# One receptance product in float32r parts, the norms' scaling on VectorE, and a planner that charges first weight loads by place

## The chip, the cores and the metric

The kernel runs on one core of a Trainium2 chip. A core has five engines that work side by side, each through its own queue in order: TensorE (PE in the profile; its weight loads are listed as PEld), VectorE (DVE), ScalarE (ACT), GpSimd (POOL) and SyncE (SP), which here issues all transfers. Products of TensorE land in PSUM, in banks of 128x512 float32. Everything else lives in SBUF, or in device memory. The metric is the time of one execution in device microseconds (us).

## What is computed

The input is x of 8 sequences by 1024 tokens by 256 channels, float32. Four blocks follow one another, each with a layer norm in front and a residual sum behind:

```python
x = x + retention(layernorm(x))      # its own norm inside, 4 heads, chunked state, gated, + its input
x = x + ffn(layernorm(x))
x = x + attention(layernorm(x))      # 16 heads, T5-style relative bias, softmax
x = x + ffn(layernorm(x))            # the same weights as the first ffn
```

The feed-forward block (ffn) mixes each token with the one before it and gates its output by a "receptance" r:

```python
xr = mu_r * x + (1 - mu_r) * x_prev
xk = mu_k * x + (1 - mu_k) * x_prev
r  = sigmoid(xr @ W_r.T)
out = r * (square(relu(xk @ W_k.T)) @ W_v.T)
```

The attention block projects q, k and v with biases, adds a bias by distance to the scores, takes a softmax over 1024 keys and projects back.

## The kernel before, in words

**Tiles and stages.** Tokens go in chunks of 256 (`CT`; four chunks, `NC`, per sequence), as tiles of 128 partitions by 2 by 256 channels. For each of 8 sequences `b` the program records: `retention(b)`, the first feed-forward block (`ffn_front`, which calls `ffn_chunk` once per chunk), `project_b` (norm and q, k, v projections of the attention), eight passes of `maxima` (scores once, for the row maximum, tiles `p`), four of `weigh` (scores again, exponentials, weighted values, tiles `s`, `e` and `acc`), and `back(b)` (output projection and the second feed-forward block, `ffn_chunk` again). So `ffn_chunk` runs 64 times: 8 sequences, 4 chunks, two blocks.

**Norms.** `moments` takes mean and variance on DVE, `rstd` and `power` the inverse root on POOL, `product` the shift. `normed` then writes the scaled tile `z` with two ACT operations of 128x256 (scale and bias per token); `turn_chunk` scales the residual `xc` the same way. `turned` transposes `z` on PE into PSUM (`ntp`, `ftp`, `btp`). In `turn_chunk` four ACT operations then read `ntp` and apply the inner norm's weights, two for the rounded part `nT[0]`, two for the full value in `z`; `nT[1]` is their difference.

**Products in two formats.** Some weights and inputs are kept as two float32r parts, a rounded one and what is left. `mm3` then makes one product from three: low by high, high by low, high by high. The projections of retention and attention (`qps`, `vps`, `gps`, `qkp`, `bvp`) are such products. Those of the feed-forward block (`kps`, `rps`, `yps`) and the output projections (`wps`, `bop`) are plain float32. `rps`, the receptance, is four float32 products of 128x256 per chunk, with tokens as the stationary operand; ACT takes its tanh.

**q and k of the attention.** In `project_b`, per chunk and per q or k, two ACT operations add the bias from PSUM into `res`, one ACT operation rounds it to the part `qk0`, and POOL (DVE for the first sequence, by `swift`) subtracts to the part `qk1`. SP then stores the parts to `stk`, from where `load_pair` brings them back per pair of heads as `q` and `k`.

**PSUM.** Seven banks under the tag `one` are shared by all products but `acc`, which has its own. A bank comes free when the last engine has read it: DVE (`pm`, `jmax`) for `p`, ACT (`e`) for `s`.

**What sets the order.** Nothing is issued as it is recorded. A planner (`Plan`) records every operation with an engine, a cost in microseconds (`estimate`; for products the argument `cost` of `mm` and `turn`), what it must wait for, and a target time. `issue` then walks a clock: whenever an engine is free in its model, it takes the ready operation with the least key (the target, plus terms for PE from `RULES`, chosen every 20 us by a hex digit of `TURNS`), places its tiles into free slots, and emits it. PE operations have a `mode`: "rows" for products over 64 partitions (`p`, `s`, `aps`), "cols" for `sps`, "acc", and "all" for the rest; a change of mode costs `SWITCH` in the model. The costs never reach the chip; they settle only the order in each engine's queue and which slot a tile gets. Tags in `SHARED` take the first free slot, other tags go round in turn.

**First loads.** `later` issues the loads of weights that come after the first of retention. Those kept in parts go through the staging tile `xo0`: ACT rounds, DVE subtracts.

Every instruction goes through one line of `emit`, line 609 in the profile of before, so groups are told apart by tile names there.

Of the kernel before, what the change touches and what calls it, by code (L numbers as in the profile page):

```python
# [10 lines left out]
F32 = mybir.dt.float32  # L11
F32R = mybir.dt.float32r
# [64 lines left out]

STRETCH = 20
TURNS = (
    "00001700f08ff825e9a10f4bfe3f7f5b737f8bc37b237273e3f16482a6fe755707160591be52e6e5"  # L80
    "788ff00f76ff5fc03fdf6bfdd4ccf65b3b9c0cf84111"
)
SWITCH = 0.1

# [94 lines left out]

SHARED = ("z", "one")
_TOUCHED = {}
LOG = None

# [126 lines left out]
class Plan:  # L312
# [14 lines left out]

    class Op:
        __slots__ = ("eng", "calls", "cost", "tail", "before", "after", "target", "mode", "news",
                     "wait", "ready", "done", "n", "tiles", "out", "group")  # L330

    def __init__(self, ctx, tc):
        self.tiles = []
# [25 lines left out]
    @staticmethod  # L359
    def estimate(eng, method, n, views, kw):  # L360
        if eng == "ACT":
            each = 600.0 if isinstance(kw.get("scale"), View) else 1200.0
            fixed = (0.055 if views[0].t.tag == "e2" else 0.045) if views[1].t.space == "psum" else 0.085
            return fixed + n / each + (0.25 if "accum_out" in kw else 0.1 if "bias" in kw and each > 600 else 0.0)
        if eng == "DVE":
            if method == "reciprocal":
                return 0.1 + n / 160.0
            if method == "tensor_scalar":
                return 0.13 + n / 1920.0

            return 0.07 + n / 960.0 + 0.055 * (method == "scalar_tensor_tensor" and kw["scalar"])
        if n <= 16:
            return 0.28 + (0.22 * n if kw.get("op") == ALU.pow else 0.0)
        if method == "affine_select":
            return 0.1 + n / 1000.0

        return 0.2 + n / (490.0 if len({id(v.t) for v in views[1:]}) > 1 else 650.0)

    def record(self, eng, real, method, args, kw):
# [5 lines left out]
        if method in ("matmul", "transpose"):  # L385
            out, group = outs[0].t, kw.pop("group", None)
            op = self.last
            if op is None or op.group is not group or group is None and op.out[0] is not out:
                op = self.new(eng)
                op.out, op.cost, op.group = [], 0.0, group  # L390
                if args[1].dtype == F32R and args[1].shape[0] == P:
                    op.cost = 0.12
                self.last = op
                k, m = args[1].shape[0], 1
                for n in args[1].shape[1:]:
                    m *= n
                op.mode = ("rows" if k == 64 and m == P else "cols") if k == 64 or m == 64 else "all"
                if out.tag == "acc":
                    op.mode = "acc"
            if out not in op.out:  # L400
                op.out.append(out)
            op.cost += cost
# [55 lines left out]
    def issue(self):  # L458
# [59 lines left out]
        while made < len(ops):  # L518
            progress = False
            for e in names:  # L520
                while free[e] <= now:
# [44 lines left out]
                    queue[e].remove(op)  # L566
                    took = op.cost
                    if e == "PE" and op.mode != mode:
                        took += SWITCH
                        mode, first = op.mode, True  # L570
                    elif e == "PE":

                        took += SWITCH * (first and mode == "rows")
                        first = False
# [38 lines left out]
def layer_kernel(ctx: ExitStack, tc: tile.TileContext, ap: dict, out: bass.AP):  # L613
# [26 lines left out]
    def mm(o, lhsT, rhs, start=True, stop=True, share=1.0, group=None):  # L640
        n = 1
        for d in rhs.shape[1:]:
            n *= d
        pe.matmul(o, lhsT, rhs, start=start, stop=stop, group=group,
                  cost=share * (0.005 + (4 if rhs.dtype == F32 else 1) * max(n, 64) / 2280.0))

    def mm3(o, lhsT, rhs, first, last):

# [65 lines left out]


    mu = const([P, 2, ND], "mu")
    wf = {k: const([P, ND, D], k) for k in ("W_r", "W_k", "W_v")}
    wb = {k: halves([P, ND, D], "b" + k) for k in ("wq", "wk", "wv")}
    wo_b = const([P, ND, D], "wo_b")
    bqk = const([P, 2, ND], "bqk")  # L720
# [12 lines left out]

    def later():
        sp.dma_start(mu, ap["f_mu"])
        for k, t in wf.items():
            sp.dma_start(t, ap["f_" + k].rearrange("(c p) n -> p c n", p=P))

        dve.tensor_scalar(wf["W_v"], wf["W_v"], 0.5, None, ALU.mult)
        for k, w in wb.items():  # L740
            t = tile2k("xo0", 2).rearrange("p (c n) -> p c n", c=ND)
            sp.dma_start(t, ap["b_" + k].rearrange("(c p) n -> p c n", p=P))
# [111 lines left out]
    def normed(xc, mv, rs, name):  # L854

        z = small([P, 2, D], "z", 2)
        nb = product(mv[:, :, 0], rs, name + "_nb")
        for n in range(2):
            act.activation(
                z[:, n], xc[:, n], AF.Identity, scale=rs[:, n : n + 1], bias=nb[:, n : n + 1]  # L860
            )
        return z

    def rows_in(ap2, c):
# [10 lines left out]
    def retention(b):  # L875
# [20 lines left out]
        def turn_chunk(c):  # L896
# [1 line left out]
            t = xc[b, c]  # L898
            z = normed(t, mv, rz, "a")
            for n in range(2):  # L900
                act.activation(
                    t[:, n], t[:, n], AF.Identity, scale=s1[:, n : n + 1], bias=m1[:, n : n + 1]
                )
            ps = turned(z, misc("ntp"))
            nT = [tile2k("nT", 2, F32R).rearrange("p (c t) -> p c t", c=ND) for _ in range(2)]
            zT = z.rearrange("p n d -> p (n d)").rearrange("p (c t) -> p c t", c=ND)
            for t in (nT[0], zT):
                for c in range(ND):
                    act.activation(
                        t[:, c], ps[:, c], AF.Identity,  # L910
                        scale=ln[:, 0, c : c + 1], bias=ln[:, 1, c : c + 1],
                    )
            swift(b == 0).tensor_tensor(nT[1], zT, nT[0], ALU.subtract)
            return nT

# [199 lines left out]
    def ffn_chunk(xt, b, ch, name, own):  # L1115
# [28 lines left out]
        def to_tokens(src, w, name):  # L1144
            ps = misc(name)
            for i in range(2):
                for c in range(ND):
# [23 lines left out]
    def project_b(b):  # L1171

        for ch in range(NC):
# [10 lines left out]
            for s, w in ((0, "wq"), (1, "wk")):  # L1184
# [6 lines left out]
                    plan.tile([P, 2, CT], F32R, f"qk{i}", f"qk{i}", 2)  # L1191
                    for i in range(NPART)
                ]
                res = plan.tile([P, 2, CT], F32, "res", "res", 1)
                step = slice(None, None, -1) if s == 0 else slice(None)
                for blk in range(2):
                    bias = bqk[:, s, blk : blk + 1]
                    act.activation(res[:, blk, step], ps[:, blk], AF.Identity, bias=bias)
                act.copy(pt[0], res)
                swift(b == 0).tensor_tensor(pt[1], res, pt[0], ALU.subtract)  # L1200
                t0 = (NC - 1 - ch if s == 0 else ch) * CT
                for p, i in enumerate((Q_PARTS, K_PARTS)[s]):
                    sp.dma_start(rows_of(s, b, t0, p), pt[i].bitcast(F32))
# [106 lines left out]
    def weigh(b, g):  # L1310
# [6 lines left out]
        for hf in (1, 0):  # L1317
# [133 lines left out]
```

## Time and profile before

| | |
|---|---|
| median of 3 runs | 2563.42 us (2562.29 to 2563.48) |
| the profiled execution | 2565.35 us, span 2563.6 us |
| granted TensorE clock, mean | 0.992 |
| busy: PE, PEld | 2477.1 us (97%), 1462.6 us (57%) |
| busy: DVE, ACT, POOL | 2100.9 us (82%), 2071.3 us (81%), 1591.6 us (62%) |
| `rps`, recorded twice for each product | 512 matmuls, 128.6 us |
| `z` on ACT, four groups | 256 operations, 150.5 us |
| bytes moved | 251.18 MB, mean 98 GB/s |

A group's line reads: source line, engine, operation, output and inputs by the program's names with shape and type, count; after the first bar the busy time in us and the mean ns of one; after the second the idle time of the engine just before them, and which work ended most of it. Busy time is the union of the recorded intervals, and the recorded intervals of neighbours can overlap a little, so the spacing of back-to-back instructions is shorter than their mean. The chain is followed backwards from the last instruction, at each step to what released it or to the instruction before it on its engine.

### The profile page before, as it was taken

To read this page: it belongs to the slowest core of one execution; us is meant where nothing else is said; L and a number is where in the kernel's file an instruction comes from. 1 tells how busy PE (TensorE), PEld (TensorE's weight loads), DVE (VectorE), ACT (ScalarE), POOL (GpSimd) and SP (SyncE) were. 2 spreads that over 40 slices of the span, in tenths; PEclk is the share of its full clock that TensorE was granted. 3 is DMA by queue.
4 is the path that set the end of the run, shared out by engine and by line. 5 is a ranking of instruction groups with operands and counts; after the bars stand their busy time and mean duration, and the time that the engine had idled before them with its cause. 6 is when DMAs were issued, how large, how long until landed. Compare 5 with 4: busy or idle time off the path is not lost.

```text
span 2563.6 us, 51515 instructions
## 1 busy us (share of the span) xinstructions
PE 2477.1 (97%) x15814; PEld 1462.6 (57%) x15814; DVE 2100.9 (82%) x6230; ACT 2071.3 (81%) x5334; POOL 1591.6 (62%) x2675
## 2 busy tenths in 40 slices
PE   5998999999999999999999999999999999999997
PEld 3886755555555556555655555555555555554555
DVE  6766988888898888888888888888888888887855
ACT  3564588898989988988889889888998888787783
POOL 3465675666666667766666676666666666665642
PEclk9999999999999999999999999999999999999999
DMA  7136132343424244433234343333243324444322
GB/s 174 42 104 150 55 92 64 92 120 99 111 74 114 78 97 119 123 82 95 71 101 110 98 109 97 89 103 89 81 115 97 101 76 132 120 114 109 92 65 67
DMA packets 252225, 251.18 MB, mean 98 GB/s; under 512 B 89042, under 2 KB 226180, under 8 KB 251924
## 3 DMA queue, kind: packets, MB, share of 16 engines
q1 hardware_dynamic: 251956, 247.89, 35.9%
q8 instruction: 132, 2.16, 0.4%
q14 instruction: 137, 1.12, 0.2%
HBM read 151.32 MB, written 98.59 MB: 97 GB/s over the span
## 4 chain that ended last, share of the span: by engine, by line
PE 78%; DVE 9%; ACT 4%; DMA 3%; POOL 3%; issue 2%; SPq 1%; POOLq 0%; DVEq 0%; ACTq 0%
PE acc L609 16%; PE p L609 10%; PE s L609 10%; PE wps L609 4%; PE yps L609 4%; PE kps L609 4%; PE rps L609 4%; PE gps L609 3%; PE qps L609 3%; DVE pm L609 3%; PE qkp L609 3%; PE vps L609 3%; PE ops L609 3%; ACT e L609 2%; PE bop L609 2%
## 5 line engine op out<-in xcount | busy, mean ns | idle before, releaser
L609 DVE TENSOR_REDUCE pm<-p 128x1 f32<-128x512 f32 (+2 forms) x2048 | 1057.7, 557 | 80.8 <-PE p L609 78.0
L609 ACT ACTIVATE e<-s 128x512 f32<-128x512 f32 (+2 forms) x2048 | 1010.6, 530 | 37.9 <-PE s L609 35.5
L609 POOL TENSOR_TENSOR e<-e,hk 128x512 f32<-128x512 f32 (+1 forms) x558 | 613.1, 1106 | 303.2 <-ACT e L609 296.5
L609 DVE CUSTOM_DVE_ANT_0 jmax<-p,hk 128x256 bf16<-128x256 f32 (+1 forms) x1152 | 427.1, 371 | 122.1 <-PE p L609 117.6
L609 PE MATMUL acc<-e,va 128*17 128x512 f32 x4096 | 524.5, 597 | 0.1
L609 PE MATMUL p<-k,q 64*128 64x512 f32 x2048 | 459.7, 438 | 10.7 <-DMA k<-stk 9.2
L609 ACT COPY e<-s 128x256 f32<-128x256 f32 (+1 forms) x1116 | 402.8, 361 | 83.3 <-PE s L609 80.3
L609 PE MATMUL s<-q,k 64*128 64x512 f32 x2048 | 453.2, 438 | 2.4 <-DVE pm L609 1.0
L609 ACT ACTIVATE e<-e 128x512 f32<-128x512 f32 (+1 forms) x576 | 336.8, 587 | 55.7 <-POOL e L609 52.9
L609 PEld LDWEIGHTS p<-k,q 64*128 64x128 f32 x2048 | 211.0, 185 | 248.2 <-ACT e L609 79.4
L609 PEld LDWEIGHTS s<-q,k 64*128 64x128 f32 x2048 | 205.2, 185 | 203.3 <-issue 63.0
L609 PEld LDWEIGHTS acc<-e,va 128*17 128x17 f32 x4096 | 79.7, 95 | 187.7 <-issue 162.1
L609 PE MATMUL rps<-W_r,xr 128*128 128x256 f32 x512 | 128.6, 393 | 12.8 <-DVE xr L609 10.6
L609 PE MATMUL yps<-W_v,xk 128*128 128x256 f32 x512 | 126.2, 389 | 4.7 <-DVE xk L609 3.4
L609 PE MATMUL wps<-wo_a,gs 128*128 128x256 f32 x512 | 127.4, 392 | 0.9 <-ACT gs L609 0.7
L609 PE MATMUL kps<-xk,W_k 128*128 128x256 f32 x512 | 125.7, 388 | 2.5 <-DVE xk L609 0.9
L609 PEld LDWEIGHTS rps<-W_r,xr 128*128 128x128 f32 x512 | 93.1, 192 | 44.3 <-issue 16.6
L609 PE MATMUL qps<-wqk,nT 128*128 128x512 f32 x384 | 109.4, 421 | 7.1 <-DVE nT L609 5.9
L609 PEld LDWEIGHTS yps<-W_v,xk 128*128 128x128 f32 x512 | 92.2, 190 | 32.1 <-issue 7.7
L609 PEld LDWEIGHTS kps<-xk,W_k 128*128 128x128 f32 x512 | 92.7, 190 | 30.5 <-issue 9.3
L609 PE MATMUL vps<-wv_a,nT 128*128 128x512 f32 x384 | 107.2, 415 | 2.4 <-DVE xc L609 1.8
L609 PEld LDWEIGHTS wps<-wo_a,gs 128*128 128x128 f32 x512 | 93.5, 192 | 25.6 <-ACT e L609 3.4
(182 smaller groups left out, 4135.5 us busy)
## 6 DMA issues: line engine op xcount, KB each, us to landing
stk<-qk SPq DMA_DIRECT2D x192, 256.0 KB
hk<-ud SPq DMA_DIRECT2D x128, 256.0 KB
q<-stk SPq DMA_DIRECT2D x128, 256.0 KB
k<-stk SPq DMA_DIRECT2D x128, 256.0 KB
od<-o SPq DMA_DIRECT2D x64, 256.0 KB
vd<-vst SPq DMA_DIRECT2D x64, 136.0 KB
va<-vd SPq DMA_DIRECT2D x32, 272.0 KB
xc<-in_x SPq DMA_DIRECT2D x32, 256.0 KB
```

The costliest lines, as they stand in the source:

```text
L609: getattr(real, method)(*[be(a) for a in args], **{k: be(a) for k, a in kw.items()})
```

## The change

Six things change.

1. `rps` becomes a product of parts. `W_r` is loaded through `xo0` and kept as two float32r tiles. A new function `parted` makes two tiles from `xr`: `xrh`, rounded, by a DVE copy, and `xrl`, what is left, by a POOL subtraction. `to_tokens` then uses `mm3`, twelve float32r products per chunk in place of four float32 ones. The four tags of the parts go into `SHARED`.
2. `normed` and the residual scaling in `turn_chunk` move from ACT to DVE, as `tensor_scalar` with two scalars per partition.
3. In `turn_chunk` ACT reads `ntp` twice, not four times; DVE copies the full value to the rounded part `nT[0]`.
4. In `project_b`, ACT writes the biased value rounded into `qk0` at once, and DVE subtracts it from PSUM plus bias into `qk1`. The tile `res`, its cast and POOL's subtraction are gone.
5. The planner's costs: DVE operations on SBUF alone, products and their shares, and a term `late` for the first load of weights that is charged when PE changes into mode "all", in place of 0.12 for every group of float32r products over 128 partitions.
6. `TURNS` has other digits.

```diff
-SHARED = ("z", "one")
+SHARED = ("z", "one", "xkh", "xkl", "xrh", "xrl")
...
-            if method == "tensor_scalar":
-                return 0.13 + n / 1920.0
+            if method in ("tensor_scalar", "tensor_copy") and all(v.t.space == "sbuf" for v in views):
+                return 0.07 + n / 1920.0 + 0.055 * kw["scalar"]
...
-                if args[1].dtype == F32R and args[1].shape[0] == P:
-                    op.cost = 0.12
...
+                op.late = (0.055 if method == "transpose" else 0.1) if op.mode == "all" else 0.0
...
-                        took += SWITCH
+                        took += SWITCH + op.late
...
-                  cost=share * (0.005 + (4 if rhs.dtype == F32 else 1) * max(n, 64) / 2280.0))
+                  cost=share * (0.004 + (4 if rhs.dtype == F32 else 1) * max(n, 64) / 2400.0))
...
-    wf = {k: const([P, ND, D], k) for k in ("W_r", "W_k", "W_v")}
+    wf = {k: halves([P, ND, D], k) if k[2] in "r" else const([P, ND, D], k) for k in ("W_r", "W_k", "W_v")}
...
-        for k, t in wf.items():
+        for k, w in wf.items():
+            parts = isinstance(w, list)
+            t = tile2k("xo0", 2).rearrange("p (c n) -> p c n", c=ND) if parts else w
             sp.dma_start(t, ap["f_" + k].rearrange("(c p) n -> p c n", p=P))
 
-        dve.tensor_scalar(wf["W_v"], wf["W_v"], 0.5, None, ALU.mult)
+            by = 0.5 if k == "W_v" else 1.0
+            if parts:
+                act.activation(w[0], t, AF.Copy, scale=by)
+                dve.scalar_tensor_tensor(w[1], t, by, w[0], ALU.mult, ALU.subtract)
+            elif by != 1.0:
+                dve.tensor_scalar(w, w, by, None, ALU.mult)
...
-            act.activation(
-                z[:, n], xc[:, n], AF.Identity, scale=rs[:, n : n + 1], bias=nb[:, n : n + 1]
-            )
+            dve.tensor_scalar(z[:, n], xc[:, n], rs[:, n : n + 1], nb[:, n : n + 1], ALU.mult, ALU.add)
...
-                act.activation(
-                    t[:, n], t[:, n], AF.Identity, scale=s1[:, n : n + 1], bias=m1[:, n : n + 1]
-                )
+                dve.tensor_scalar(t[:, n], t[:, n], s1[:, n : n + 1], m1[:, n : n + 1], ALU.mult, ALU.add)
...
-            for t in (nT[0], zT):
-                for c in range(ND):
-                    act.activation(
-                        t[:, c], ps[:, c], AF.Identity,
-                        scale=ln[:, 0, c : c + 1], bias=ln[:, 1, c : c + 1],
-                    )
+            for c in range(ND):
+                act.activation(
+                    zT[:, c], ps[:, c], AF.Identity, scale=ln[:, 0, c : c + 1], bias=ln[:, 1, c : c + 1]
+                )
+            dve.tensor_copy(nT[0], zT)
...
+        def parted(t, name):
+            hi, lo = (plan.tile([P, ND, CT], F32R, name + part, name + part, 1) for part in "hl")
+            dve.tensor_copy(hi, t)
+            pool.tensor_tensor(lo, t, hi.bitcast(F32), ALU.subtract)
+            return [hi, lo]
+
+        xrs = parted(xr, "xr")
...
-                    mm(ps[:, i * D : (i + 1) * D], src[:, c, i * P : (i + 1) * P], w[:, c],
-                       c == 0, c == ND - 1)
+                    if isinstance(w, list):
+                        mm3(ps[:, cols], [t[:, c, t0] for t in src], [t[:, c] for t in w], c == 0, c == ND - 1)
+                    else:
+                        mm(ps[:, cols], src[:, c, t0], w[:, c], c == 0, c == ND - 1)
...
-        rps = to_tokens(xr, wf["W_r"], "rps")
+        rps = to_tokens(xrs, wf["W_r"], "rps")
...
-                res = plan.tile([P, 2, CT], F32, "res", "res", 1)
                 step = slice(None, None, -1) if s == 0 else slice(None)
                 for blk in range(2):
                     bias = bqk[:, s, blk : blk + 1]
-                    act.activation(res[:, blk, step], ps[:, blk], AF.Identity, bias=bias)
-                act.copy(pt[0], res)
-                swift(b == 0).tensor_tensor(pt[1], res, pt[0], ALU.subtract)
+                    hi, lo = (t[:, blk, step] for t in pt)
+                    act.activation(hi, ps[:, blk], AF.Identity, bias=bias)
+                    dve.scalar_tensor_tensor(lo, ps[:, blk], bias, hi, ALU.add, ALU.subtract)
...
-            mm(ps[hh] if isinstance(ps, list) else ps[:, hh, :], a, m, share=0.5, group=group)
+            mm(ps[hh] if isinstance(ps, list) else ps[:, hh, :], a, m, share=0.525, group=group)
...
-                       es[j // 2][:, j % 2, :], n == 0, n == NT - 1, share=0.243)
+                       es[j // 2][:, j % 2, :], n == 0, n == NT - 1, share=0.2535)
```

More of the change, by code (lines that the diff above doesn't have):

```diff
@@ L79 @@
 TURNS = (
-    "00001700f08ff825e9a10f4bfe3f7f5b737f8bc37b237273e3f16482a6fe755707160591be52e6e5"
-    "788ff00f76ff5fc03fdf6bfdd4ccf65b3b9c0cf84111"
+    "000b20007f00479b33fc0e3159e1394fb7f1b55d193e708b478ffd9a17afd2fd8bfc952df2d66fdc"
+    "dfe689773d7351bdfdf597f9d9e973450fbff1111"
 )
@@ L329 @@
         __slots__ = ("eng", "calls", "cost", "tail", "before", "after", "target", "mode", "news",
-                     "wait", "ready", "done", "n", "tiles", "out", "group")
+                     "wait", "ready", "done", "n", "tiles", "out", "group", "late")
     def __init__(self, ctx, tc):
@@ L1146, in to_tokens @@
             for i in range(2):
+                cols, t0 = slice(i * D, (i + 1) * D), slice(i * P, (i + 1) * P)
                 for c in range(ND):
-                    mm(ps[:, i * D : (i + 1) * D], src[:, c, i * P : (i + 1) * P], w[:, c],
-                       c == 0, c == ND - 1)
+                    if isinstance(w, list):
+                        mm3(ps[:, cols], [t[:, c, t0] for t in src], [t[:, c] for t in w], c == 0, c == ND - 1)
+                    else:
+                        mm(ps[:, cols], src[:, c, t0], w[:, c], c == 0, c == ND - 1)
             return ps
-        rps = to_tokens(xr, wf["W_r"], "rps")
+        rps = to_tokens(xrs, wf["W_r"], "rps")
         er = xr.rearrange("p c t -> p (c t)")
```

## The prediction, made before the changed kernel ran

> **What bounds the kernel now.** I read first the page's shares of busy time and its chain, then the stretches, then the chain in one window, where equal work in two number formats stands side by side, then the groups of VectorE (DVE), ScalarE (ACT) and GpSimd (POOL), and last the waits of TensorE's weight loads.
>
> The page (busy time, then the chain that ended last):
>
> ```profile
> PE 2477.1 (97%) x15814; PEld 1462.6 (57%) x15814; DVE 2100.9 (82%) x6230; ACT 2071.3 (81%) x5334; POOL 1591.6 (62%) x2675
> ...
> PE 78%; DVE 9%; ACT 4%; DMA 3%; POOL 3%; issue 2%; SPq 1%; POOLq 0%; DVEq 0%; ACTq 0%
> ```
>
> TensorE (PE) is busy 97%; only 86.5 us of 2563.6 are not. The stretches (us and busy us of PE, PEld, DVE, ACT, POOL, each with its instructions; then clock, DMA share, GB/s) say where: at both ends, hardly in the middle, where DVE and ACT stand level at 88%.
>
> ```profile
> 0.00:64.00 64.00, 34.42 (x152) 24.85 (x153) 40.77 (x96) 22.41 (x46) 20.65 (x63) 0.92 0.72 174
> 640.00:960.00 320.00, 318.25 (x2079) 175.46 (x2078) 281.81 (x855) 282.64 (x746) 206.59 (x321) 1.00 0.36 94
> 2500.00:2564.00 64.00, 46.36 (x218) 34.32 (x214) 33.06 (x73) 20.08 (x41) 18.40 (x46) 0.95 0.21 65
> ```
>
> So work taken off PE counts nearly in full, as long as DVE and ACT keep freeing its seven PSUM banks. The chain at 679 us (start, length, work):
>
> ```profile
> 679.43 0.24 PE s L609 x2
> 679.67 1.57 PE bvp L609 x12
> 681.25 0.98 PE acc L609 x8
> ...
> 682.89 0.23 PE p L609 x2
> 683.12 1.92 PE rps L609 x8
> 685.05 0.43 PE s L609 x2
> ```
>
> `rps` is the receptance's product, four float32 products of 128x256 (each recorded twice). `bvp` is the same size, tokens stationary, as twelve float32r products: exactly the form that `rps` takes. Both stand between the same neighbours.
>
> Groups by form (busy us, mean ns | idle before):
>
> ```profile
> L609 DVE SCALAR_TENSOR_TENSOR xr<-xk,mu,zT 128x256 f32<-128x256 f32 x128 | 75.8, 621 | 16.5 <-POOL xo L609 13.8 <-POOL xk L609 2.4
> L609 DVE TENSOR_TENSOR gs<-gs,ops 128x256 f32<-128x256 f32 x128 | 48.7, 413 | 16.1 <-ACT sq L609 10.6 <-PE ops L609 5.0
> L609 DVE TENSOR_SCALAR wo_a<-wo_a,gn 128x1024 f32<-128x1024 f32 x1 | 0.7, 733 | 0.0
> L609 DVE TENSOR_SCALAR W_v<-W_v 128x512 f32<-128x512 f32 x1 | 0.4, 444 | 0.0
> L609 ACT ACTIVATE z<-xc,b_nb,b_y 128x256 f32<-128x256 f32 x64 | 37.7, 630 | 10.6 <-POOL b_nb L609 10.4 <-POOL nT L609 0.2
> L609 POOL TENSOR_TENSOR qk<-res,qk 128x512 fp32r<-128x512 f32 x56 | 72.9, 1301 | 39.6 <-ACT qk L609 36.4 <-DVE xk L609 2.7
> ```
>
> The first two DVE rows have one size; the one whose tensors both lie in SBUF takes 621 ns, the one with a tensor in PSUM 413. The timeline near the start shows what lies behind this:
>
> ```profile
> 13.79 0.20 POOL L609 TENSOR_TENSOR a_m<-a_mv,a_y 128x2 f32<-128x2 f32 x1
> ...
> 17.11 0.73 DVE L609 TENSOR_SCALAR wo_a<-wo_a,gn 128x1024 f32<-128x1024 f32 x1
> 17.32 0.58 POOL L609 TENSOR_TENSOR a_m<-a_mv,a_y 128x2 f32<-128x2 f32 x1
> ```
>
> The same tiny POOL operation takes 0.20 us alone and 0.58 under a DVE operation from SBUF, ending just after it: the two engines exclude each other there.
>
> Waits of weight loads (total, times, longest):
>
> ```profile
> PEld p L609 <- ACT e L609: 79.4, 135, 0.9
> PEld p L609 <- DVE pm L609: 55.2, 74, 0.9
> PEld s L609 <- DVE pm L609: 43.1, 82, 0.9
> PEld s L609 <- ACT e L609: 29.4, 51, 0.9
> ```
>
> ACT and DVE hold PE's banks about equally: 109 against 98 us, mostly hidden under running products.
>
> **The change, part by part.**
>
> *Receptance.* 64 chunks go from 1.92 to 1.57 us: -0.35 each, -22.4 us. (By busy time: 128.6 us now, 768 products at 51.4/384 = 0.134 make 102.8, so -25.8; I take the smaller.) The order of PE's instructions leaves the number of changes between kinds of product as it is (1937 before, 1939 after), so that price doesn't move. In this order `kps` stands ahead of `rps` in all 64 chunks, where `rps` came first in 59.
>
> *Its parts.* 64 DVE copies of 128x512 from SBUF (`xrh`), between 0.444 (`W_v`, same size) and 0.69 (two-operand rows such as `xr<-xr,yps`, 686 ns); I take 0.444, also one operand in SBUF: 28 us. 64 POOL subtractions at 1.30 (`qk`): 83 us. `rps` now waits for copy, subtraction and two hand-overs, some 2.1 us; `kps`, now ahead of it (1.73 us from its start to the next product's in the tail), covers most of it. Behind it on PE's in-order queue wait the next `s` and `p`.
>
> *Norms on DVE.* ACT loses 256 `z` (37.8+37.7+37.6+37.4 = 150.5 us) and 64 residual scalings (38.1). DVE gains 320 operations of 128x256; 733 against 444 ns gives 289 per 512 elements, so 0.30 each: 96 us.
>
> *nT and q/k.* ACT loses 64 `nT` (34.8) and 64 casts of `res` (40.4); DVE gains 32 copies at 0.444 (14 us). POOL loses 56 subtractions (72.9), DVE 8 (5.5), and DVE gains 128 subtractions of 128x256 from PSUM, between 0.413 (`gs`) and 0.621 (`xr`); I take 0.413, one operand in PSUM: 53 us. A bank of `qkp` is held about 0.8 us longer, one of `ntp` freed two ACT operations earlier.
>
> *Exclusion.* 416 new DVE operations read SBUF alone. The `xr` row averages 0.621 against 0.44 in an undisturbed pair (0.88 for two in the last chunk), so 0.18 is lost to POOL; for shorter operations I take 0.15: 62 us. Ends: 0, and 0.38 as POOL's 0.58 against 0.20 has it: 158 us.
>
> Sums. DVE: 28+96+14+53-5.5+62 = +248 us (ends 185 and 400), to some 2350. ACT: -264, to 1807. POOL: +10. None of the three is PE, so they cost by what PE waits for them. By the weight loads' waits, ACT's 109 us shrink by 264/2071 = 13% (-14) and DVE's 98 grow by 248/2101 = 12% (+12): -2. By the chain instead: DVE's 9% (231 us) grows by 27, ACT's 4% (103 us) shrinks by 13: +14. I take -2, as those rows are PE's own waits; the other is an end. The other end: half of the 2% of `e` on ACT in the chain, -25.
>
> The Trainium skill's page "SBUF — State Buffer", section "SBUF: two separate sides", says that DVE and GpSimd take a shared pair of ports as an exclusive lock for a whole instruction. It speaks against this change. POOL's 0.58 agrees. If each new operation came at random into POOL's (62% busy, about 1 us each, half of one left on average), it would wait 0.3 us: an estimate of 125 us in place of 62, and by the same waits the forecast would rise by 3 us.
>
> *Edges.* The load of `W_r` moves on SP's queue from place 14 to 24, behind `W_k`, `W_v`, `wo_b`, both `Wg`, four small loads and both `c_stat`; those ahead of `bps` come one 256 KB load earlier, those of `wk`, `wv` go behind 17 stores of `kr`. First `rps` is at 82.6 us and first `qkp` at 100, so the late ones are covered (bare, they would cost some 5 us). `bps` starts PE at 17.2 us; a load earlier is about -1, and `ntp` no longer waits behind `ups`: -2 together. In the last four chunks `rps` now fills the 1.41 us in which `yps` waits for `xk`'s square, but waits itself for `xrl`: about -0.5 each, -2. The two added operations for `W_r`'s parts lie in that slack: nothing; bare, 1.3 us.
>
> *Costs and turns* only reorder; their effect lies in the ends of the wait term.
>
> Sum: -22.4 - 2 - 2 - 2 = -28.4. The profiled execution took 2565.35 us (span 2563.6 and 1.75 around it), so it would take 2537; the median lies 1.9 below it: 2535.
>
> **Rivals.**
> A, the forecast (0.52): 2535, own range 2517 to 2555.
> B, ACT's relief is worth more (0.19): -25 instead of -2, 2512, and as much as 2500. For it: pieces of 2 to 4 us of ACT `e` on the chain. Against: DVE must then keep up at over 90%.
> C, the gain goes into new waits (0.17): `xrl` comes late. POOL has a queue of 1.3 us operations ahead, and if 1 us is bare in a third of the chunks, 21 us return: 2556; this case reaches from 2545 to 2572 and includes that the change does nothing for the end.
> D, slower (0.12): DVE becomes the bound. In 640 to 960 us it has 38 us to spare; +248 over the run is +31 there, and at +305 it is full. At +400 (single-rate copies, long exclusion) the 95 us above go onto the path in about three quarters of the span: 2535+71 = 2606. With half of that excess it is 2571.
>
> **How the numbers follow.** A difference under 0.2%, 5 us, can't be told from none. Likeliest is A: 2535. Leaving out B's lower half and D with its upper part gives 2505 to 2573. Faster: A 0.51, B 0.19, C 0.09: 0.79. Same: A 0.01, C 0.06: 0.07. Slower: D 0.12, C 0.02: 0.14.
>
> **What would show it.** `rps` with 768 products between `s` and `p` at 1.57 on the chain; DVE at 2300 to 2400 us, ACT near 1810; `z` on DVE at 0.30 alone and 0.4 to 0.5 on average; few us of PE waiting for POOL `xrl`. Wrong if `rps` keeps 1.9, if `p` waits for DVE `pm` far more than 100 us, or if PE's idle time in the middle changes by over 20 us.

## The result and the profile after

The changed kernel takes 2607.26 us (2601.66 to 2611.72, four executions) beside 2562.86 for the kernel before: a ratio of 1.017, 95% interval 1.0155 to 1.0185. It is 44 us slower, where the prediction had 28 us less. The profiled execution took 2609.54 us with a span of 2607.8, against 2565.35 and 2563.6. Every instruction now goes through line 608.

Page of the changed kernel, busy time and chain, in the columns of the lines of before:

```profile
PE 2492.1 (96%) x16070; PEld 1471.8 (56%) x16070; DVE 2329.8 (89%) x6767; ACT 1880.6 (72%) x4887; POOL 1617.3 (62%) x2683
...
PE 63%; DVE 27%; DMA 3%; issue 2%; POOL 2%; ACT 2%; SPq 0%; DVEq 0%; POOLq 0%; ACTq 0%
```

VectorE's share of the chain went from 9% to 27%, three times as much for 11% more work; TensorE's fell from 78% to 63%. The stretches, one more of 20 us added:

```profile
0.00:64.00 64.00, 32.05 (x145) 23.01 (x146) 43.30 (x103) 16.27 (x32) 16.34 (x52) 0.89 0.72 174
640.00:960.00 320.00, 310.59 (x2043) 176.03 (x2035) 291.37 (x864) 250.92 (x668) 202.68 (x314) 0.99 0.33 87
...
680.00:700.00 20.00, 18.20 (x111) 10.19 (x103) 19.96 (x49) 14.71 (x38) 15.08 (x20) 1.00 0.07 14
```

In the second stretch TensorE was busy 318.25 of 320 us before and is busy 310.59 now: the loss is in the middle of the run, not at its ends. Over 640 to 1920 us it is 1244.2 of 1280 where it was 1273.3. Counted from the start of each product to the start of the next, TensorE spends 18.8 us more than before on `p`, 18.8 on `s` and 13.8 on `acc`, 18.8 less on `rps` and 15.7 less on `yps`.

The granted clock has a part in this. In the trace it is 1.0 or 0.5 and nothing between; in the changed kernel products of `qkp` start 213 ns apart at 0.5 and 118 apart at 1.0. The clock is at 0.5 for 43 us of the run before and for 63 us of the run after, and within 640 to 1920 us for none before and 20 after. That is worth some 10 of the 44 us at most, an estimate from half of those 20. Three of these stretches follow stops of TensorE (1.9 us at 980, 2.0 at 1391, 2.7 at 1906) during which VectorE is busy 98 to 100%. That a stop brings the low clock about is not shown.

VectorE, by the line of the second stretch, is still idle for 29 of the 320 us. The last line shows why that mean misleads: in these 20 us VectorE is busy 19.96 and TensorE 18.20. The chain there (start, length, work):

```profile
680.22 1.20 DVE pm L608 x2
681.42 0.84 DVE xr L608
682.26 0.33 DVE jmax L608
682.60 0.68 DVE pm L608 x3
683.27 0.33 DVE jmax L608
...
684.57 0.39 DVE xk L608
684.96 1.20 DVE pm L608 x2
686.16 0.39 DVE xk L608
686.55 0.34 DVE xrh L608
```

For six microseconds the chain never leaves VectorE: it works through a backlog, and TensorE follows. The groups of the new work (busy us, mean ns | idle before):

```profile
L608 DVE TENSOR_SCALAR z<-xc,f_y,f_nb 128x256 f32<-128x256 f32 x64 | 37.6, 622 | 3.0 <-POOL f_nb L608 2.9
L608 DVE TENSOR_SCALAR z<-xc,a_y,a_nb 128x256 f32<-128x256 f32 x64 | 34.1, 566 | 0.5 <-POOL a_nb L608 0.4
L608 DVE TENSOR_SCALAR xc<-xc,a_s,a_m 128x256 f32<-128x256 f32 x64 | 33.9, 551 | 0.0
L608 DVE CAST xrh<-xr 128x512 fp32r<-128x512 f32 x64 | 28.5, 445 | 0.5 <-PE rps L608 0.5
L608 DVE SCALAR_TENSOR_TENSOR qk<-qkp,bqk,qk 128x256 fp32r<-128x256 f32 x128 | 56.8, 476 | 6.2 <-ACT qk L608 5.8
...
L608 PE MATMUL rps<-W_r,xrl 128*128 128x256 f32 x256 | 79.0, 308 | 2.0 <-POOL xrl L608 0.5 <-POOL xk L608 0.4 <-DVE pm L608 0.4
```

The 320 scalings (five such groups) average 585 ns. The receptance's products hardly wait for `xrl` (0.5 us in the whole run), and they are as quick as forecast; the chain at 1018 us:

```profile
1018.37 0.23 PE p L608 x2
1018.60 1.60 PE rps L608 x12
```

So each part of the change costs or saves on its own engine roughly what was forecast, and the sum still has the wrong sign. The experiments ask where the 44 us come from, and what became of the receptance's 22.

### The profile page after: what moved, and what is told of

Its sections match the earlier page's. It is cut to its first block, busy times and chain, and to the rows that moved or that the text cites. A ratio compares the mean times of both kernels' runs of the same rounds, so it can differ in the third digit from the quotient of the medians.

```text
span 2607.8 us, 52068 instructions
## 1 busy us (share of the span) xinstructions
PE 2492.1 (96%) x16070; PEld 1471.8 (56%) x16070; DVE 2329.8 (89%) x6767; ACT 1880.6 (72%) x4887; POOL 1617.3 (62%) x2683
## 4 chain that ended last, share of the span: by engine, by line
PE 63%; DVE 27%; DMA 3%; issue 2%; POOL 2%; ACT 2%; SPq 0%; DVEq 0%; POOLq 0%; ACTq 0%
PE acc L608 13%; DVE pm L608 10%; PE s L608 9%; PE p L608 8%; DVE jmax L608 3%; PE yps L608 3%; PE wps L608 3%; PE rps L608 3%; DVE z L608 3%; PE gps L608 3%; PE kps L608 3%; PE ops L608 2%; PE qkp L608 2%; PE qps L608 2%; PE vps L608 2%
## 5 line engine op out<-in xcount | busy, mean ns | idle before, releaser
L608 PE MATMUL acc<-e,va 128*17 128x512 f32 x4096 | 531.2, 601 | 5.8 <-ACT e L608 5.6
L608 PE MATMUL p<-k,q 64*128 64x512 f32 x2048 | 471.7, 439 | 12.3 <-issue 3.5
L608 PE MATMUL s<-q,k 64*128 64x512 f32 x2048 | 469.7, 441 | 9.7 <-DVE pm L608 6.8
L608 ACT COPY e<-s 128x256 f32<-128x256 f32 (+1 forms) x1116 | 395.0, 354 | 116.4 <-PE s L608 113.7
L608 ACT ACTIVATE e<-e 128x512 f32<-128x512 f32 (+1 forms) x576 | 329.9, 575 | 83.9 <-POOL e L608 78.5
L608 PEld LDWEIGHTS s<-q,k 64*128 64x128 f32 x2048 | 211.8, 185 | 217.6 <-issue 66.4
L608 PE MATMUL kps<-xk,W_k 128*128 128x256 f32 x512 | 129.9, 397 | 17.4 <-DVE xk L608 14.1
L608 POOL TENSOR_TENSOR ta<-ta,tb 128x256 f32<-128x256 f32 x112 | 82.9, 748 | 48.1 <-DVE tb L608 45.6
L608 POOL TENSOR_TENSOR ao_y<-ao_a,mhalf 128x4 f32<-128x4 f32 x64 | 67.3, 1052 | 62.1 <-DVE ao_a L608 60.6
L608 PE MATMUL gps<-wg_a,nT 128*128 128x512 f32 x384 | 105.4, 409 | 0.4 <-DVE pm L608 0.2
```

The lines of the kernel that those rows point to most:

```text
L608: getattr(real, method)(*[be(a) for a in args], **{k: be(a) for k, a in kw.items()})
```

## Experiments

### First, one part undone at a time

`TURNS` has one digit per 20 us of the planner's clock, 124 before and 121 after, and each picks the terms by which TensorE's next product is chosen. The first four kernels keep such digits as they stand:

```diff
u_norms:   the changed kernel, `normed` and the residual scaling back on act.activation
u_rps:     the changed kernel, one float32 product again
-        xrs = parted(xr, "xr")
-        rps = to_tokens(xrs, wf["W_r"], "rps")
+        rps = to_tokens(xr, wf["W_r"], "rps")
...
plan_only: the operations of before, with the changed costs and digits
turns_old: the changed kernel with the digits of before
```

Norms back on ScalarE:

> The changed kernel with the norms' scaling (z and the residual) back on ACT, all else as changed, planned anew. Theory V (DVE sets the pace: 320 operations from SBUF, 177 us of DVE with what they lose to POOL): the time falls by 35 to 60 us, to 2550 to 2570; DVE's share of the chain falls from 27% to near 10%. Rival O (the order that the new costs and turns give is what costs): stays within 12 us of 2607. Rival X (the receptance's low part comes late from POOL): stays near 2600.

Receptance back to float32:

> The changed kernel with the receptance in float32 again, all else as changed. Theory V: PE has 22 us more, DVE 28 us less, so 2600 to 2620. Rival X: the waits go with the parts, 2570 to 2590. Rival O: near 2607 as well, so this run tells X from the other two.

Operations of before under the changed costs and digits:

> The kernel before with the changed planner's costs and turns and none of the changed operations. Theory V and rival X: 2563 to 2580, as before but for a less fitting order. Rival O: 2590 to 2610, as the changed kernel.

Digits of before:

> The changed kernel with the old digits of TURNS, which shows how much the order alone moves the time. Theory V: 2600 to 2630, since the pace is DVE's whatever the order. Rival O: moves by more than 25 us either way.

Measured: 2688.34 (ratio 1.050, 1.0484 to 1.0516), 2684.09 (1.0484, 1.0467 to 1.0500), 2668.18 (1.0419, 1.0403 to 1.0434) and 2728.33 (1.0658, 1.0641 to 1.0676). All four are 61 to 121 us slower than the changed kernel itself, and no theory had such numbers, except that rival O's condition for `turns_old` (more than 25 us either way) is met. Even `plan_only`, which computes what the kernel before computes, is 107 us slower than it. The digits fit one list of operations and costs; a kernel that differs by one edit and keeps them is measured with an order made for another. These runs say nothing of the parts. From here on each list gets digits of its own, from one search in the planner's clock.

### One part undone, with digits of its own

```diff
norms_act_fit: the changed kernel, norms on ACT, own digits
-            dve.tensor_scalar(z[:, n], xc[:, n], rs[:, n : n + 1], nb[:, n : n + 1], ALU.mult, ALU.add)
+            act.activation(
+                z[:, n], xc[:, n], AF.Identity, scale=rs[:, n : n + 1], bias=nb[:, n : n + 1]
+            )
...
plan_fit:      the operations of before, changed costs, own digits
rps_f32_fit:   u_rps with own digits
z_charged_fit: the changed kernel, z charged 0.50 us in the planner, own digits
-                return 0.07 + n / 1920.0 + 0.055 * kw["scalar"]
+                return (0.5 if method == "tensor_scalar" and n == 256 else 0.07 + n / 1920.0 + 0.055 * kw["scalar"])
```

> The changed kernel with the norms' scaling back on ACT, as u_norms, but with TURNS digits searched anew for this list of operations (121 digits, the same length as in the changed kernel), since old digits on a new list cost 100 us and more. Theory V (VectorE's new operations from SBUF hold up the chip in a way that the plan doesn't see): 2530 to 2570, 40 to 75 us under the changed kernel, with DVE's share of the chain near 10%. Rival O (the new costs of products and first loads make a plan that PE can't keep): 2595 or more.

> The operations of before under the changed planner's costs, digits searched anew for them (122 digits). Theory V: 2540 to 2570, so the costs themselves do no harm. Rival O: 2590 to 2610.

> The changed kernel with the receptance in float32 again, digits searched anew (121). Theory V: 2600 to 2625, since PE has 22 us more and DVE's scalings stay. Rival X (the parts' waits cost): 2570 to 2590.

> The changed kernel with one number of the planner changed: the 320 scalings on DVE are charged 0.50 us each, about what they take in the changed kernel's profile with POOL in the way, and not 0.26; digits searched anew (122). Theory V in the form that the plan's blindness costs: 2560 to 2590, 15 to 45 us under the changed kernel. Theory V in the form that DVE is simply full: 2600 to 2620. Rival O: 2600 to 2620.

Measured: `norms_act_fit` 2563.11 (1.0003, 0.9991 to 1.0015), `plan_fit` 2553.17 (0.9974, 0.9961 to 0.9987), `rps_f32_fit` 2603.64 (1.0166, 1.0145 to 1.0187), `z_charged_fit` 2633.66 (1.0284, 1.0260 to 1.0307). Busy time and chain of `norms_act_fit`:

```profile
PE 2467.3 (96%) x16070; PEld 1467.4 (57%) x16070; DVE 2197.7 (86%) x6447; ACT 2011.3 (78%) x5207; POOL 1604.4 (63%) x2683
...
PE 76%; DVE 13%; ACT 4%; DMA 4%; issue 2%; POOL 1%; SPq 0%; DVEq 0%; POOLq 0%; ACTq 0%
```

Theory V's ranges hold for the first three; the fourth lies above all that were given. With the norms on ScalarE the 44 us are gone, and VectorE's share of the chain falls from 27% to 13%. The costs as such do no harm: `plan_fit` is not slower than the kernel before. A planner that is told a price nearer the measured one of `z` does not mend the loss (`z_charged_fit` takes 2634, and 2629 is what the same list takes uncharged with digits of the same search, `after_fit` below). The receptance in parts gives nothing in the company of the other edits: 2604 without, 2607 with.

### The norms alone, and how much digits move

```diff
norms_dve_fit: plan_fit with the norms' scaling on DVE, own digits
after_fit, before_fit: the two kernels as they are, digits of my search
```

> The operations of before, with the norms' scaling alone moved to VectorE (receptance, nT and the parts of q and k as before), the changed kernel's costs, digits searched for it. Beside it stands the same without the move: 2553.2, VectorE 2108 us. Theory V (time follows VectorE's busy time along one curve: 2108 us 2553, 2161 us 2554, 2198 us 2563, 2314 us 2600, 2330 us 2607): VectorE some 2275 us here, so 2577 to 2592. Rival W (the move costs its 44 us whatever else VectorE does, as z comes late for the turning that follows it): 2592 to 2602. Rival R (the move pays where VectorE has room, since ScalarE loses 200 us): 2553 or less.

> The changed kernel with digits of my search. If digits of another search move the time by little (what the comparisons of fitted kernels assume): 2600 to 2615 (2607 with its own). If the 44 us are in the digits it was given: 2580 or less.

> The kernel before, its own costs, digits of my search. Same assumption: 2553 to 2572 (2562 with its own).

Measured: 2606.61 (1.0195, 1.0169 to 1.0221), 2629.10 (1.0283, 1.0262 to 1.0305) and 2571.45 (1.0055, 1.0040 to 1.0070).

```profile
PE 2491.9 (96%) x15814; PEld 1466.6 (56%) x15814; DVE 2254.8 (87%) x6550; ACT 1934.2 (74%) x5014; POOL 1599.3 (61%) x2675
...
PE 70%; DVE 18%; DMA 5%; ACT 3%; POOL 3%; issue 2%; SPq 1%; POOLq 0%; DVEq 0%; ACTq 0%
```

The page of `norms_dve_fit`, above, has VectorE at 87%, 147 us over `plan_fit`'s 2108.1. The move alone costs 53 us (2553 to 2607), more than theory V's curve had (2577 to 2592) and a little above rival W's range. The control of the changed kernel misses as well: a second search moves it by 22 us. That of the kernel before stays just inside its range, moved by 9 (13 from the 2558.41 of the kernel before beside it). So some 9 to 22 us is the margin of every comparison across two orders here: the norms' 44 and 53 us exceed it, the receptance's 3 to 9 don't. The miss of V's curve, 15 us, doesn't either. (With `after_fit`, whose digits come from the same search as the others', in place of the changed kernel, the norms cost 66 us and the parts of the receptance 25.)

### The load alone, in one order

To separate load from order, three kernels share digits and the order on every engine. The base is `norms_act_fit`'s list with four idle VectorE operations at each of 160 places where a norm's rows are at hand. They are charged 0.20 us each, and nothing reads what they write (they share the tile `jmax`, which is no longer planned in these three).

```diff
+    def idle_load(src):
+        dve.tensor_reduce(spare[:, 0:1], src, AX.X, ALU.add, cost=0.2)                 # d_red_fit
+        dve.tensor_scalar(spare, src, ln[:, 0, 0:1], ln[:, 1, 0:1], ALU.mult, ALU.add, cost=0.2)   # d_ts_fit
...
+        for n in range(4):
+            idle_load(xc[:, n // 2, n % 2 * P : (n % 2 + 1) * P])
...
+            if method == "tensor_reduce" and not isinstance(args[0], View):            # d_none: planned, not issued
+                continue
```

> The change with the norms' scaling on ScalarE (2563.11), and 640 idle reductions of 128 x 128 from SBUF added on VectorE, ten to each norm's two tiles of rows less six; they write one junk column that nothing reads. Each is charged 0.20 us in the planner; digits searched for this list of operations. Theory V (what lengthens the run is the work that VectorE is given, whatever its kind: +132 us of it went with +44 us of time): some +128 us on VectorE, so 2563 + 43 = 2606, between 2595 and 2620. Theory L (it is not the work but the port of SBUF that VectorE's operations on SBUF alone share with GpSimd, and a reduction does not lengthen beside GpSimd): 2563 to 2578, and a reduction of some 0.2 us with or without GpSimd at work. Theory F (what the change loses it loses by ScalarE's work moved earlier or later, not by VectorE's load): 2563 within 6.

> The same 640 places, the same order on every engine and the same digits as in the kernel with reductions, but each idle operation is a scaling with two scalars from SBUF, 128 x 128, the form of z in the changed kernel. Theory V: as the reductions, within 8 us of that kernel plus the difference of the two durations times 640 times one third. Theory L: 2600 to 2615, and at least 20 us above the kernel with reductions; the scaling alone 0.20 to 0.25 us and 0.30 to 0.45 beside GpSimd, GpSimd's own operations on two tiles longer too.

> The kernel with 640 idle reductions, the same digits and the same order on every engine, but the reductions are not issued (their places in the plan stay empty). So three kernels of one order: no idle work, 178 us of reductions (2599.8), 316 us of scalings (2712.2). Theory V (about a third of a microsecond for each microsecond that VectorE is given, 0.84 near the top): 2599.8 - 0.31 x 178 = 2545, between 2535 and 2563. Rival O (the 37 us over the kernel with the norms on ScalarE were the order, not the load): 2590 or more.

Measured: `d_none` 2574.32 (1.0059, 1.0044 to 1.0074), `d_red_fit` 2599.78 (1.0147, 1.0129 to 1.0164), `d_ts_fit` 2712.22 (1.0582, 1.0559 to 1.0605). The chains by engine, in that order of kernels, each a fence of its own:

```profile
PE 80%; DVE 8%; DMA 4%; ACT 4%; POOL 2%; issue 2%; SPq 1%; DVEq 0%; POOLq 0%; ACTq 0%
```

```profile
PE 69%; DVE 18%; DMA 4%; ACT 3%; issue 3%; POOL 2%; SPq 1%; DVEq 0%; POOLq 0%; ACTq 0%
```

```profile
PE 51%; DVE 35%; issue 5%; DMA 3%; ACT 3%; POOL 2%; SPq 1%; DVEq 0%; POOLq 0%; ACTq 0%
```

The idle operations, of `d_red_fit` and then of `d_ts_fit`:

```profile
L611 DVE TENSOR_REDUCE jmax<-xc 128x1 f32<-128x128 f32 x512 | 142.8, 279 | 10.3
L611 DVE TENSOR_REDUCE jmax<-xo 128x1 f32<-128x128 f32 x128 | 35.6, 278 | 2.1
```

```profile
L611 DVE TENSOR_SCALAR jmax<-xc,ln 128x128 f32<-128x128 f32 x512 | 239.5, 468 | 10.9
L611 DVE TENSOR_SCALAR jmax<-xo,ln 128x128 f32<-128x128 f32 x128 | 76.7, 599 | 2.3
```

Hardly anything waits for these operations; they mostly only occupy VectorE. They read rows that ScalarE scales in place afterwards, and by the profile all waits that they end come to 12.6 us in `d_red_fit` and 12.7 in `d_ts_fit`. So part of the first step below can be such waits, hardly any of the second. 178 us of reductions add 25.5 us, 0.14 us for each. Replacing each by a scaling of the same size adds 138 us of VectorE's time and 112 us to the run, 0.82 for each. So load that hardly anything waits for lengthens the run before VectorE is full (85% to 89%), and the next step costs several times as much for each microsecond. The granted clock has a share: it is at 0.5 for 62, 38 and 93 us of the three profiled executions, and with half of that time taken off each the two prices would be some 0.19 and 0.68 (an estimate). The second step differs from the first in kind too, as it brings pieces of more than 1 us, so the runs don't tell a price that rises with the load from a price of long pieces. Theory V had the reductions' time (2595 to 2620) but not what it rests on: it has 0.31 for each microsecond in both steps, where 0.14 and 0.82 came, so `d_none` and `d_ts_fit` (some 2646 by V) missed; rival O's 2590 or more for `d_none` missed too. Theory F's 2563 missed. Theory L's number for the reductions alone (2563 to 2578) missed and so did its 2600 to 2615 for the scalings; that they stand at least 20 us above the reductions is met, with 112.

The trace says where the scalings' length comes from. Sorted by whether GpSimd had work during the instruction, the reduction takes 0.279 us in both cases. The scaling takes 0.341 us alone (247 of 640) and 0.590 beside GpSimd (393): half of these take no longer than alone (median 0.348), one in ten 1.18 or more.

### ScalarE's relief, in one order

```diff
z_act_order: norms_dve_fit, its digits and TensorE's order; when the instructions are issued,
+            if method == "tensor_scalar" and isinstance(args[2], View) and isinstance(args[3], View):
+                o, i, m, a = (be(v) for v in args[:4])
+                self.tc.nc.scalar.activation(o, i, AF.Identity, scale=m, bias=a)
+                continue
```

> The kernel with the norms' scaling alone on VectorE (2606.6), the same digits and TensorE's order word for word, but each of the 320 scalings is issued on ScalarE, at the place in the program where VectorE had it. VectorE some 176 us less, ScalarE some 196 us more. Theory V: 2606.6 - 0.31 x 176 = 2552, between 2540 and 2570. Rival O (the order made for that plan costs the 53 us): 2600 or more. Rival S (ScalarE's queue, planned without them, holds the exponentials back): above 2575 with TensorE's waits on ScalarE's e up.

Measured: 2625.44 (1.0261, 1.0239 to 1.0282), 19 us slower than with the scalings on VectorE. Chain, and the waits of weight loads (total us, times, longest):

```profile
PE 67%; ACT 13%; DVE 8%; DMA 5%; POOL 4%; issue 2%; SPq 1%; POOLq 0%; ACTq 0%; DVEq 0%
```

```profile
PEld p L613 <- ACT e L613: 87.4, 150, 1.3
PEld s L613 <- ACT e L613: 45.5, 84, 0.9
```

VectorE's share falls to 8%, as theory V has it, but ScalarE's rises from 3% to 13%, and TensorE's loads wait 133 us for its exponentials by these two rows, where `norms_dve_fit` has 112. That is rival S (O's bound is met as well): an order made for one placement doesn't suit the other. So the run doesn't tell how much of the 53 us is VectorE's load and how much the order that goes with it; that stays open.

### The receptance with the norms on ScalarE, and more of the work moved back

```diff
na_rps32_fit: norms_act_fit, receptance by one float32 product, own digits
best1_fit:    norms_act_fit, nT's second reading and the copy xrh on ACT, own digits
-            dve.tensor_copy(hi, t)
+            act.copy(hi, t)
```

> The change with the norms' scaling on ScalarE and the receptance by one float32 product again (16 products of 256 columns in place of 24 of a quarter of the passes; no copy of xr, no subtraction on GpSimd, no parts of W_r). Digits searched. My forecast's step on the products (that they save 0.35 us in each of 64 places on the path, 22 us, where VectorE has room): 2563 + 22 = 2585, between 2576 and 2594. Rival (that the saving is eaten by the work that feeds it, as it was with the norms on VectorE, 2604 against 2607): 2557 to 2568.

> The change with the norms' scaling, the two copies of nT and the rounded copy of xr all on ScalarE, so that VectorE carries some 45 us less than with the norms on ScalarE alone and ScalarE some 60 us more; the products of parts stay. Digits searched. Theory V (one third of VectorE's work is paid): 2563 - 15 = 2548, between 2538 and 2556, below the kernel before (2562.9). Theory F or a bound by ScalarE: 2563 or above.

Measured: 2553.80 (0.9967, 0.9956 to 0.9978) and 2583.89 (1.0083, 1.0067 to 1.0099). The forecasts for `na_rps32_fit` both missed; for `best1_fit` theory V missed, and "2563 or above" is met. Without the parts the kernel is 9 us quicker than with them, not 22 slower. On TensorE the saving is there: summed from the start of each product to the start of the next work, the receptance takes 125.4 us in `na_rps32_fit` and 105.4 in `norms_act_fit`. But the page of `na_rps32_fit` has VectorE at 2161.1 us, 37 less, and TensorE changes 50 times less between kinds of product. What of the 20 us goes into VectorE's load and what into the order, the runs don't tell; 9 us are within the margin of the digits. `best1_fit` has VectorE as low (2162.1 us) and ScalarE at 2073.5, and is 21 us slower than `norms_act_fit`, about the margin: relief of VectorE alone showed no gain while ScalarE filled.

The kernels with digits of their own, by VectorE's busy time:

| kernel | norms on | receptance | DVE, ACT busy, us | time, us |
|---|---|---|---|---|
| before | ACT | float32 | 2101, 2071 | 2562.9 |
| `plan_fit` | ACT | float32 | 2108, 2067 | 2553.2 |
| `before_fit` | ACT | float32 | 2112, 2071 | 2571.5 |
| `na_rps32_fit` | ACT | float32 | 2161, 2016 | 2553.8 |
| `best1_fit` | ACT | parts | 2162, 2074 | 2583.9 |
| `norms_act_fit` | ACT | parts | 2198, 2011 | 2563.1 |
| `norms_dve_fit` | DVE | float32 | 2255, 1934 | 2606.6 |
| `rps_f32_fit` | DVE | float32 | 2305, 1877 | 2603.6 |
| after | DVE | parts | 2330, 1881 | 2607.3 |
| `z_charged_fit` | DVE | parts | 2340, 1876 | 2633.7 |
| `after_fit` | DVE | parts | 2349, 1877 | 2629.1 |

All six kernels with the norms on ScalarE lie below 2585 us, all five with them on VectorE above 2603. Two kernels come out below both given ones, by 6 to 7 us against the kernel before beside them, which is within the margin of the digits: `plan_fit`, the operations of before under the changed costs, and `na_rps32_fit`, which keeps the shorter handling of `nT`, `q` and `k`.

## Why the prediction was wrong

**What bounds the kernel: the step that failed.** "As long as DVE and ACT keep freeing its seven PSUM banks" was the condition, and it was examined on means over 320 us. Rival D put the point where VectorE decides at +305 us, where such a stretch would be full. The measured load stayed below it (+229 by the page, with 29 us idle in that stretch), and the run was slower all the same. The load comes in bursts. Joining VectorE's busy intervals where at most 0.1 us lies between, the joined stretches longer than 10 us come to 544 us before and 1282 after; those over 20 us to 53 and 568. (In the kernels of one order, those over 10 us: 545 without idle work, 1014 with reductions, 1318 with scalings.) VectorE was full for 20 us at a time and TensorE fell behind in such a stretch, as shown above, while VectorE's mean over 320 us was 91%. How long seven banks last was not measured. Among the kernels with digits of their own these stretches come to 544 to 796 us with the norms on ScalarE and to 1002 to 1475 with them on VectorE. They don't predict the time across all orders: `plan_only`, with digits made for another list, has 418 us of them and takes 2668.

**The wait term, "-2 (ends -25 and +14)".** This is the term that was mis-sized. With the receptance at its measured -18.8 us and the edges near nothing (both below), the 44 us leave +63 for it, 65 off; the new order and the clock are in this figure too. The term scaled four rows of waits of weight loads by the growth of each engine's busy time, and after the change these rows came out nearly as scaled (total us, times, longest):

```profile
PEld p L608 <- ACT e L608: 68.1, 109, 1.6
PEld p L608 <- DVE pm L608: 67.0, 98, 1.7
PEld s L608 <- DVE pm L608: 45.2, 89, 1.4
PEld s L608 <- ACT e L608: 29.0, 51, 1.7
```

VectorE's two make 112 us for 98, ScalarE's 97 for 109, +2 together. What failed is that they were taken for the price of the waits, though the prediction had called them mostly hidden under running products. The time was lost beside them: by the profile TensorE's products themselves waited 61.8 us for VectorE where it was 30.7, and `p`, `s` and `acc` took 51 us more from start to start. The other end, by the chain, had +27 us for VectorE's share; it went from some 231 to some 704 us for 11% more work. The idea that ScalarE's relief pays for VectorE's load failed with it. ScalarE lost 191 us by the page (294 by the sum of its groups; recorded intervals overlap) and the time rose.

**Receptance, -22.4.** Nearly right in size: 1.60 us on the chain for 1.57, and 18.8 us over the 64 chunks from start to start (20.0 with the norms on ScalarE) for 22.4. (`bvp` stood between `s` and `acc`, `rps` between `p` and `s`, so their neighbours were not the same; the size held all the same.) The saving doesn't show in the time with the norms on either engine. Rival C had the saving lost, but in another way: there are 0.5 us of waiting for `xrl`. The hand-over that did show is `kps` waiting 14.1 us for `xk`, since `kps` now goes first; before, `rps` waited 10.6 us for `xr` in that place.

**VectorE's sum.** Forecast +248, measured +273 by the sum of its groups and +229 as the page counts. Within it: copies `xrh` 28.5 us for 28, `nT` 16.9 for 14, the subtractions of q and k 56.8 for 53. The scalings take 0.585 us each on average, where 0.30 and 0.15 for exclusion were given. Alone `z` takes 0.405 as recorded (0.325 from start to start when back to back), so the base was low by 0.1; the loss to GpSimd is 0.18, for 0.15. The Trainium skill's page "SBUF — State Buffer", section "SBUF: two separate sides", with its lock for a whole instruction, had led to an estimate of 0.3 us per operation. That was a mean over all operations, and the measured mean is 0.18 (0.19 for `z`), nearer to the forecast's own 0.15. The lock itself agrees with the trace: the 159 of 256 `z` beside GpSimd take 0.708 us on average for 0.405 alone, but half of them 0.44 or less and one in ten 1.37 or more.

**Edges, -4.** The start came as forecast: the longest wait of TensorE, for `bv`, is 15.9 us after 17.2, and the first `qps` comes 1.3 us earlier. In the last chunks `rps` does fill the wait of `yps`, but `kps` now waits up to 3.9 us for `xk` (`rps` waited up to 3.3 for `xr` in that place). From the last `acc` to the end it is 55.1 us after 54.0, so both ends together came to about nothing.

**Costs and turns "only reorder".** They do, but an order is worth more than any term of the sum: with digits made for another list the four first kernels took 80 to 125 us more than the same lists with digits of their own, and another search of the same list moved 9 to 22. That was no part of the prediction's range, and the forecast's 28 us were hardly larger than it.

**Rival D** names the side and, by chance, nearly the number (2606 for its +400 us); its mechanism, a VectorE that is full over hundreds of microseconds, isn't what the trace shows. Its chance of 0.12 was too small, because every other case took the mean load for the limit.

**The signs.** `rps` at 1.60 us, VectorE's 2330 us and the 0.5 us for `xrl` came as named. `z` took 0.405 us alone and 0.59 on average where 0.30 and 0.4 to 0.5 were named, and ScalarE's busy time was 1881 us for 1810. Of the signs of being wrong, TensorE's idle time in the middle showed, up by 29 us over 640 to 1920 us; `p`'s wait for `pm` did not (67.0 us after 55.2).

## What to carry to other kernels

An engine at 82% on average isn't 18% free: before work is moved to it, measure how long it is already busy without a gap, against how much its consumers have in reserve, and price added work by a run with idle operations of the very form, in the same order. Where an order is fitted to a list of operations, undoing one edit needs a new fit, and the difference between two fits of one list is the least effect that such a comparison can show. A saving on the busiest engine that is fed by work on the second busiest isn't a saving until both are counted.

## What was not expected of the hardware

- The exclusion is paid by VectorE, nearly alone. GpSimd's `e` with `hk` takes 1292 ns beside 640 scalings and 1293 beside 640 reductions, and its busy time is 1616.3 and 1613.1 us, while the scaling rises from 0.341 to 0.590 us. From the one `a_m` of 0.58 us the prediction had thought it mutual.
- A reduction from SBUF isn't held up by GpSimd at all (0.279 us with and without), a scaling with two scalars of the same 128x128 is. Theory L had expected that of the reduction. The two take 0.279 and 0.341 us alone, 0.279 and 0.590 in company.
- Relief of ScalarE by 191 us showed no gain while VectorE's load rose, and loading ScalarE again, in an order not made for it, cost 19 us although VectorE was relieved.
